# Seven whole-row taps of the last VectorE tile and three of the first TensorE conv tile, computed on ScalarE and added by accumulating transfers

## The chip, the core and the metric

The kernel runs on one core of one Trainium2 chip. A core has five engines with one instruction queue each: TensorE (PE in the profile; PEld is its weight load), VectorE (DVE), ScalarE (ACT), GpSimd (POOL) and SyncE (SP, which here only issues transfers). The engines meet through semaphores, and each queue is worked off in order: an instruction that waits holds all those behind it on its engine. Data lies in an on-chip memory of 128 partitions, matmuls write to a small accumulator memory (PSUM), and 16 DMA engines move the rest. The metric is the device time of the whole program in microseconds (us), as the median of several runs.

## What is computed

The input is x with the shape (16, 384, 32, 32): 16 images, 384 channels, 32 x 32 pixels, float32. Two residual layers follow each other; each starts with a group norm over 32 groups.

```
x = x + attention(group_norm(x))        # 8 heads of 48 channels over 1024 tokens, then a projection
w_sym = (w + rot90(w) + rot180(w) + rot270(w)) / 4
x = x + depthwise_conv_7x7(group_norm(x), w_sym, padding 3)
```

The depthwise convolution multiplies each channel with its own 7 x 7 weights, so it is a sum of 49 products, one for every shift (dy, dx) from -3 to 3, each of a shifted picture with one weight per channel. These 49 terms are called taps here. A tap with dx = 0 shifts only whole rows: it reads and writes one run of 1024, 992, 960 or 928 neighbouring values in each partition, with no gaps at row ends.

## The kernel before

**Tiles.** Channels lie on partitions, so an image is three tiles k = 0, 1, 2 of 128 channels x 1024 pixels. For every image b the attention runs on TensorE: `qk_step` (L418), `v_step` (L444), `s_step` (L469, scores, with the exponential on ScalarE at L477), `av_step` (L485) and the projection (L538, in the last image `proj_part`, L575). The result x1 (`x1s[b, k]`) is normalised into xn1 (`xn1s[b, k]`, by `conv_begin` through `Stats.apply`, L336 and L340), and the convolution adds its 49 taps onto x1, which is then stored. In the profile these names appear without digits: x is x1, xn is xn1, sum is sum2.

**Who does the convolution.** For images 0 to 13 VectorE does all 49 taps of all three tiles, one instruction per tap (`conv_tap`, L600), in turn over the active tiles so that neighbours on the queue write to different tiles. These taps fill VectorE while TensorE works on the attention of the next image. For the last two images TensorE helps with three tiles (`PE_TILES`): tile (14, 2), then (15, 2) and (15, 1). There remain (14, 0), (14, 1) and (15, 0) for VectorE; (15, 0) is called `LONE`. As taps of one tile alone would depend on each other, `tap_of_two` lets the taps of `LONE` go alternately to x1 and to a second sum `sum2`, which is started by a product at L858 and added to x1 at the end (L866). The tile is then stored by one GpSimd transfer (`conv_end`, L610).

**Convolution on TensorE.** A normalised tile is stored to DRAM (`conv_store`, L674) and loaded back in shifted copies, in two row halves h with two parts a each (`conv_load`, L681; four transfers per part, in the tail of the program two on SP and two on ScalarE's queue). `conv_on_pe` (L704) then runs, for each half, 14 taps (d0, dx), each standing for four dy: d0 = 0 holds dy = -3 to 0, d0 = 1 holds dy = 1 to 3 (and one row of zeros). Each is four matmuls of 32 output columns in the program, eight in the profile, where a float32 matmul shows as two. The pieces in which they are issued lie in `pe_conv`, filled in `x1_chains`. For (14, 2) and (15, 2) ScalarE then copies the PSUM tile (L719), an accumulating GpSimd transfer adds it to x1 (L720), and a second transfer stores x1. For (15, 1), the last one, VectorE adds the halves straight from PSUM (`conv_on_pe_half`, L727), and each half is stored by itself (L728).

**What sets the order.** The instruction order on each engine is written out by the program itself, as a planner that keeps two model clocks, `clock` for TensorE and `vclock` for VectorE. `after(wait, cost, f)` puts a piece of work into the queue `later`, due at a model time; `catch_up(to)` emits due pieces and between them as many taps as the model says fit before `to`. `applies` holds work for ScalarE, which `act_slot` emits where TensorE leaves it room. The order is fixed at build time; at run time only semaphores act. In the last image `fast_finish` (the projection's second half, the division, the statistics of x1) and `fast_end` follow; then the loop at L1253 alternates pieces of the TensorE convolution with VectorE work until nothing is left. `opool`, `npool` and `epool` are rings of 6, 6 and 8 tiles: a new tile takes the place of the oldest of its ring and waits until that is free.

Of the kernel before, what the change touches and what calls it, by code (L numbers as in the profile page):

```python
# [44 lines left out]
def kernel(  # L45
# [25 lines left out]
    nc = tc.nc  # L71

    B, C, H, W = x.shape
    N = H * W
    NK = C // P
# [3 lines left out]
    HALF = N // 2  # L79
    KS = w_conv.shape[2]  # L80
    PAD = KS // 2
# [12 lines left out]
    wsym = consts.tile([P, NK, KS, KS], F32, name="wsym")  # L94
# [15 lines left out]
    def run(general):  # L110
        tag = "g" if general else "f"
        with ExitStack() as stack:
# [23 lines left out]
            xns, x1s, qks, os_, accs, es, xn1s = {}, {}, {}, {}, {}, {}, {}  # L136
# [2 lines left out]

            PE_TILES = [(B - 2, PE_K[0])] + [(B - 1, k) for k in PE_K]  # L140
            LONE = (B - 1, 0)

            def flat(t):
                return t.rearrange("p h n -> p (h n)")
# [25 lines left out]
            late, pps = {}, {}  # L170
# [415 lines left out]
                )  # L586


            def region(*ds):
                return [(slice(max(0, -d), H - max(0, d)), slice(max(0, d), H - max(0, -d))) for d in ds]  # L590

            def conv_begin(st, b, k, engine):
                xn1s[b, k] = npool.tile([P, N], F32, tag="xn1", name=f"xn1_{b}_{k}")
                st.apply(xn1s[b, k], x1s[b, k], k, engine)

            def conv_tap(b, k, dy, dx, dst=None):
                (oy, iy), (ox, ix) = region(dy, dx)
                dst = x1s[b, k] if dst is None else dst
                acc = dst.rearrange("p (h w) -> p h w", w=W)[:, oy, ox]
                nc.vector.scalar_tensor_tensor(  # L600
                    acc,
                    xn1s[b, k].rearrange("p (h w) -> p h w", w=W)[:, iy, ix],
                    wsym[:, k, dy + PAD, dx + PAD : dx + PAD + 1],
                    acc,
                    ALU.mult,
                    ALU.add,
                )

            def conv_end(b, k):
                nc.gpsimd.dma_start(  # L610
                    out[b, k * P : (k + 1) * P].rearrange("p h w -> p (h w)"), x1s.pop((b, k))
                )
# [63 lines left out]
            def conv_load(b, k, h, a):  # L676
# [11 lines left out]
                    )  # L688
                shs[b, k, h, a] = t

            def conv_on_pe(b, k, h, first, last):
                if (b, k) not in pss:
                    pss[b, k] = psum(f"ps_conv_{b}_{k}")
                order = sorted(
                    ((d0, dx) for d0 in range(2) for dx in range(-PAD, PAD + 1)),
                    key=lambda t: t[1] != 0,
                )
                for n, (d0, dx) in enumerate(order):
                    if not first <= n < last:
                        continue  # L700
                    _, (ox, ix) = region(0, dx)
                    for i in range(SH):
                        src = shs[b, k, h, i // 2][:, i % 2, 0 : ROWS * W]
                        nc.tensor.matmul(  # L704
                            pss[b, k][CH * i : CH * (i + 1), h, :].rearrange(
                                "p (y x) -> p y x", x=W
                            )[:, :, ox],
                            lhsT=mats[k][:, i, d0 * KS + dx + PAD, :],
                            rhs=src.rearrange("p (y x) -> p y x", x=W)[
                                :, SH * d0 : SH * d0 + H // 2, ix  # L710
                            ],
                            start=(n == 0),
                            stop=(n == len(order) - 1),
                        )

            def conv_on_pe_end(b, k):
# [53 lines left out]
            if general:  # L770
                for b in range(B):
                    if b:
                        load_x(b)
                    st = Stats(f"x_{b}")
# [18 lines left out]
                    st = Stats(f"x1_{b}")  # L793
# [17 lines left out]
            clock, vclock, last_image, catching = 0.0, 0.0, 1e9, False  # L811
            later, count = [], 0
# [18 lines left out]

            def tap():

                while len(active) < NK and chains:
                    active.append([*chains.popleft(), 0])
                if not active:
                    return 0.0
                b, k, n = active[0]
                if (b, k) == LONE:
                    active.append(active.pop(0))  # L840
                    return tap_of_two(b, k, active[-1])
                took = us_tap(*TAPS[n])
                conv_tap(b, k, *TAPS[n])
                c = active.pop(0)
                c[2] += 1
                if c[2] < len(TAPS):
                    active.append(c)
                else:
                    conv_end(b, k)
                return took  # L850

            def tap_of_two(b, k, c):

                n = c[2]
                c[2] += 1
                if n == 1:
                    late["sum2"] = opool.tile([P, N], F32, tag="o", name=f"sum2_{b}_{k}")
                    nc.vector.tensor_scalar(  # L858
                        late["sum2"], xn1s[b, k], wsym[:, k, PAD, PAD : PAD + 1], None, ALU.mult
                    )  # L860
                elif n < len(TAPS):

                    tn = n if n > 1 else 1
                    conv_tap(b, k, *TAPS[tn], late["sum2"] if n % 2 else None)
                else:
                    nc.vector.tensor_tensor(x1s[b, k], x1s[b, k], late["sum2"], ALU.add)  # L866
                    active.remove(c)
                    conv_end(b, k)
                return (950 + 128) / 955

            def catch_up(to):
                nonlocal vclock, catching
# [47 lines left out]
            applies = deque()  # L920
# [142 lines left out]
            st = Stats("x_0")  # L1063
# [56 lines left out]
            def conv_piece():  # L1120
                nonlocal clock
                b, k, h, first, last = pe_conv.popleft()
                while (b, k, h, 1) not in shs and pe_loads:
                    loads(1)
                conv_on_pe(b, k, h, first, last)
                clock += 6.2 * (last - first) / KS
                if last == 2 * KS:
# [48 lines left out]
            for b, n0, size in [  # L1176
# [74 lines left out]
            vclock = clock  # L1251
# [57 lines left out]
```

## Time and profile before

| what | value |
|---|---|
| time, median of 3 runs | 2926.08 us (2924.81 to 2926.97) |
| time of the profiled execution | 2926.36 us |
| its span (first to last instruction) | 2924.6 us |
| TensorE busy | 2895.0 us, 99% |
| VectorE busy | 2580.3 us, 88% |
| ScalarE busy | 1441.0 us, 49% |
| GpSimd busy | 254.2 us, 9% |
| last matmul of the attention's projection ends | 2832.1 us |
| last matmul of the convolution ends | 2906.3 us |
| last VectorE instruction ends | 2915.0 us |

All times inside an execution are counted from the start of its span. The busy share of an engine is a mean over the whole program; the changed code runs in the last 220 us, of which the last 80 us, after the attention of image 15, matter most. So the answers of the trace for these windows say more than the totals.

### The profile page before, as it was taken

How to read it: one execution, taken by the hardware profiler on the slowest of the kernel's cores; microseconds unless marked ns; L12 is line 12 of the kernel's file. 1: busy time of each engine (PE TensorE's matmuls, PEld its weight loads, DVE VectorE, ACT ScalarE, POOL GpSimd, SP SyncE). 2: the span in 40 equal slices, each digit the busy share in tenths (PEclk: the TensorE clock that was granted, in tenths of full speed). 3: DMA queues.
4: the chain of work that ended last, by engine and by line, in shares of the span. 5: the costliest groups of instructions: out<-in, count | busy, mean ns of one | idle time of the engine just before them, and what ended most of it. 6: DMA issues, size and time to landing. Idle time of an engine off the chain costs nothing.

```text
span 2924.6 us, 30111 instructions
## 1 busy us (share of the span) xinstructions
PE 2895.0 (99%) x11442; PEld 1164.5 (40%) x11442; DVE 2580.3 (88%) x2571; ACT 1441.0 (49%) x1721; POOL 254.2 (9%) x400
## 2 busy tenths in 40 slices
PE   8999999999999999999999999999999999999997
PEld 4343343433434343343433434343343434434332
DVE  5312999989899898999989899898999989899988
ACT  2545445464454655445464454556445464554520
POOL 3111004010100101000010100101010010100000
PEclk9999999999999999999999999999999999999999
DMA  7422022120312203012220302203022220302314
GB/s 281 131 29 62 16 35 76 37 68 23 68 29 43 69 21 84 16 35 69 42 63 23 72 29 39 70 21 84 16 41 64 43 62 24 80 24 35 104 53 128
DMA packets 72059, 168.93 MB, mean 58 GB/s; under 512 B 30288, under 2 KB 32224, under 8 KB 70368
## 3 DMA queue, kind: packets, MB, share of 16 engines
q0 software_dynamic: 32688, 109.34, 14.7%
q1 hardware_dynamic: 37936, 54.94, 7.4%
q10 hardware_dynamic: 1280, 2.62, 0.3%
q8 instruction: 92, 1.51, 0.2%
q14 instruction: 63, 0.52, 0.1%
HBM read 118.61 MB, written 28.72 MB: 50 GB/s over the span
## 4 chain that ended last, share of the span: by engine, by line
PE 92%; issue 5%; DVE 2%; DMA 0%; POOL 0%; ACT 0%; POOLq 0%
PE ps_s L469 29%; PE acc L485 29%; PE ps_qk L418 17%; PE ps_v L444 9%; PE ps_proj L538 8%; DVE x L600 1%; DVE sum L600 1%; DMA x<-in_x 0%; PE warm L1060 0%; PE ps_st_x L308 0%; ACT qk L425 0%; POOL v L180 0%; POOL qk L434 0%; POOL sc_x L329 0%; POOL x L1241 0%
## 5 line engine op out<-in xcount | busy, mean ns | idle before, releaser
L600 DVE SCALAR_TENSOR_TENSOR x<-xn,wsym,x 128x899 f32<-128x899 f32 (+9 forms) x2181 | 2375.7, 1162 | 138.7 <-ACT xn L340 138.7
L477 ACT ACTIVATE e<-ps_s 128x1024 f32<-128x1024 f32 x1024 | 952.4, 1051 | 52.2 <-PE ps_s L469 49.1
L469 PE MATMUL ps_s<-qk 48*128 48x512 f32 x4096 | 914.8, 596 | 1.3 <-ACT qk L425 1.1
L485 PE MATMUL acc<-e,v 128*64 128x512 f32 x4096 | 907.2, 595 | 0.0
L469 PEld LDWEIGHTS ps_s<-qk 48*128 48x128 f32 x4096 | 375.9, 185 | 536.4 <-ACT e L477 259.6
L485 PEld LDWEIGHTS acc<-e,v 128*64 128x64 f32 x4096 | 283.0, 137 | 608.2 <-issue 600.8
L418 PE MATMUL ps_qk<-x,wqk 128*128 128x512 f32 x1152 | 508.7, 598 | 2.4 <-DVE x L336 2.4
L496 ACT COPY o<-acc 128x512 f32<-128x512 f32 x128 | 75.1, 587 | 604.7 <-PE acc L485 604.7
L418 PEld LDWEIGHTS ps_qk<-x,wqk 128*128 128x128 f32 x1152 | 217.2, 191 | 290.1 <-issue 287.6
L444 PE MATMUL ps_v<-wv,x 128*128 128x384 f32 x768 | 252.0, 488 | 0.0
L538 PE MATMUL ps_proj<-o,wp 128*128 128x512 f32 x540 | 234.2, 592 | 0.0
L425 ACT COPY qk<-ps_qk 128x1024 f32<-128x1024 f32 x96 | 96.9, 1009 | 263.6 <-PE ps_qk L418 263.6
L553 POOL DMA_DIRECT2D x<-in_x x45 | 39.4, 875 | 1803.0 <-ACT x L546 1424.3
L444 PEld LDWEIGHTS ps_v<-wv,x 128*128 128x128 f32 x768 | 144.6, 190 | 109.6 <-ACT e L477 12.1
L538 PEld LDWEIGHTS ps_proj<-o,wp 128*128 128x128 f32 x540 | 102.6, 190 | 126.0 <-issue 119.6
L453 ACT COPY v<-ps_v 128x384 f32<-128x384 f32 x128 | 55.1, 483 | 185.5 <-PE ps_v L444 185.5
L546 ACT ACTIVATE x<-ps_proj,bp 128x1024 f32<-128x1024 f32 x45 | 50.2, 1114 | 182.7 <-PE ps_proj L538 182.7
L521 DVE TENSOR_TENSOR o<-o,inv 128x1024 f32<-128x1024 f32 x63 | 76.8, 1219 | 51.0 <-DMA inv<-inv 46.5
L340 ACT ACTIVATE xn<-x,sc_x 128x1024 f32<-128x1024 f32 x46 | 53.8, 1231 | 80.3 <-DMA sc_x<-gr_x 57.0
L704 PE MATMUL ps_conv<-sh,mat 128*32 128x464 f32 (+3 forms) x672 | 69.2, 570 | 1.9 <-DVE x L727 1.9
L363 DVE BATCH_NORM_STATS2 bs_all<-xs 128x6 f32<-128x512 f32 x84 | 52.2, 683 | 18.2 <-DMA xs<-in_x 18.2
L510 DVE RECIPROCAL rec<-sums 128x16 f32<-128x16 f32 x63 | 15.3, 243 | 53.6 <-DMA sums<-sum 53.5
(123 smaller groups left out, 556.6 us busy)
## 6 DMA issues: line engine op xcount, KB each, us to landing
x<-in_x POOLq DMA_DIRECT2D x90, 512.0 KB, 5.6
inv<-inv SPq DMA_DIRECT2D x126, 256.0 KB
out<-x POOLq DMA_DIRECT2D x47, 512.0 KB, 3.8
xs<-in_x POOLq DMA_DIRECT2D x42, 512.0 KB, 6.5
qk<-qk POOLq DMA_DIRECT2D x96, 128.0 KB, 5.8
o<-o SPq DMA_DIRECT2D x90, 64.0 KB
sh<-xd SPq DMA_DIRECT2D x32, 160.0 KB
x<-in_x SPq DMA_DIRECT2D x6, 512.0 KB
```

Of the source, the lines that this page charges most:

```text
L418: nc.tensor.matmul(ps[:, h, :], lhsT=wqk[:, k, s, t, :], rhs=xns[b][:, k, h * HALF : (h + 1) * HALF], start=(k == 0), stop=(k == NK - 1),)
L425: nc.scalar.copy(halves(qks[u][:, s, :]), ps)
L444: nc.tensor.matmul(ps[:, j, 0:C], lhsT=xns[b][:, k, t * P : (t + 1) * P], rhs=wv[:, k, :], start=(k == 0), stop=(k == NK - 1),)
L453: nc.scalar.copy(dst.rearrange("p (h d) -> p h d", d=D + 1)[:, :, 0:D], ps[:, j, 0:C].rearrange("p (h d) -> p h d", d=D),)
L469: nc.tensor.matmul(ps[:, j, :], lhsT=qks[u][r, 1, i * P : (i + 1) * P], rhs=qks[u][r, 0, h * HALF : (h + 1) * HALF], start=True, stop=True,)
L477: nc.scalar.activation(es[n], ps, AF.Exp, scale=SCALE)
L485: nc.tensor.matmul(accs[u, h][64 * j : 64 * j + 64, :], lhsT=v_of(u, i, j), rhs=e[:, j, :], start=(i == 0), stop=(i == NT - 1),)
L496: nc.scalar.copy(os_[u][:, h * HALF : (h + 1) * HALF], accs.pop((u, h)))
L521: nc.vector.tensor_tensor(os_[u], os_[u], invs.pop(u), ALU.mult)
L538: nc.tensor.matmul(ps[:, h, :], lhsT=wp[:, t, o * P : (o + 1) * P], rhs=os_[NP * b + t][:, h * HALF : (h + 1) * HALF], start=(t == 0), sto ...
L600: nc.vector.scalar_tensor_tensor(acc, xn1s[b, k].rearrange("p (h w) -> p h w", w=W)[:, iy, ix], wsym[:, k, dy + PAD, dx + PAD : dx + PAD + 1],
L704: nc.tensor.matmul(pss[b, k][CH * i : CH * (i + 1), h, :].rearrange("p (y x) -> p y x", x=W)[:, :, ox], lhsT=mats[k][:, i, d0 * KS + dx + ...
```

## The change

It takes the dx = 0 taps of two tiles off the engines that did them, and it stores the last tile in another way.

- `ROWS_ONLY` names the taps: dy = 1, 2, 3 of tile (14, 2), which is TensorE's first, and all seven dy of `LONE`. `taps_of` and `pe_taps` leave them out of VectorE's and TensorE's lists; on TensorE that is the one pair (d0, dx) = (1, 0) in each of the two halves.
- `product` computes such a tap on ScalarE: one `activation` with a per-channel scale over a run of whole rows. For tile (14, 2) `rows_early` puts three products into `applies`; they write into the tiles in which xn1 of image 15 will lie later (`spare`), and GpSimd transfers with `accum_op=ALU.add` add them to x1 of (14, 2).
- For `LONE`, `lone_sums` writes the product dy = 0 into `sum2` and dy = 1 into a third sum `sum3`; `lone_rows` writes the other five into five tiles of `epool`, and `add_step` issues five accumulating transfers into `sum3`, planned 8 us apart.
- The end of `LONE` becomes: `sum2 += sum3`, then `x1 += sum2` in two halves, each stored by its own transfer, one on SP and one on ScalarE's queue, in place of one addition and one GpSimd transfer.
- In the last image xn1 of tile 0 is computed by ScalarE and no longer by GpSimd.
- `vclock -= 5.0` in `x1_chains` of image 14 lets the planner put more taps ahead of the other VectorE work that follows.

```diff
+            ROWS_ONLY = {PE_TILES[0]: (1, 2, 3), LONE: range(-PAD, PAD + 1)}
+            def taps_of(b, k):
+                return [t for t in TAPS if t[1] or t[0] not in ROWS_ONLY.get((b, k), ())]
...
+            def product(dst, b, k, dy):
+                rows, src = ((slice(i.start * W, i.stop * W)) for i in region(dy)[0])
+                nc.scalar.activation(
+                    dst[:, rows],
+                    xn1s[b, k][:, src],
+                    AF.Identity,
+                    scale=wsym[:, k, dy + PAD, PAD : PAD + 1],
+                )
+                return dst[:, rows], rows
...
             def conv_begin(st, b, k, engine):
-                xn1s[b, k] = npool.tile([P, N], F32, tag="xn1", name=f"xn1_{b}_{k}")
+                xn1s[b, k] = spare.pop((b, k), None) or new_xn1(b, k)
...
+            PE_TAPS = [(d0, dx) for d0 in range(2) for dx in range(-PAD, PAD + 1)]
+            PE_TAPS.sort(key=lambda t: t[1] != 0)
+            def pe_taps(b, k):
+                return [t for t in PE_TAPS if t != (1, 0) or (b, k) not in ROWS_ONLY]
...
             def tap_of_two(b, k, c):
                 n = c[2]
                 c[2] += 1
-                if n == 1:
-                    late["sum2"] = opool.tile([P, N], F32, tag="o", name=f"sum2_{b}_{k}")
-                    nc.vector.tensor_scalar(
-                        late["sum2"], xn1s[b, k], wsym[:, k, PAD, PAD : PAD + 1], None, ALU.mult
-                    )
-                elif n < len(TAPS):
-                    tn = n if n > 1 else 1
-                    conv_tap(b, k, *TAPS[tn], late["sum2"] if n % 2 else None)
+                taps = taps_of(b, k)
+                if n < len(taps):
+                    conv_tap(b, k, *taps[n], late["sum2"] if n % 2 else None)
+                elif n == len(taps):
+                    assert not adds
+                    dst = late["sum2"]
+                    nc.vector.tensor_tensor(dst, dst, late["sum3"], ALU.add)
                 else:
-                    nc.vector.tensor_tensor(x1s[b, k], x1s[b, k], late["sum2"], ALU.add)
+                    for h in range(2):
+                        cols = slice(h * HALF, (h + 1) * HALF)
+                        dst = x1s[b, k][:, cols]
+                        nc.vector.tensor_tensor(dst, dst, late["sum2"][:, cols], ALU.add)
+                        (nc.sync, nc.scalar)[h].dma_start(
+                            out[b, k * P : (k + 1) * P].rearrange("p h w -> p (h w)")[:, cols], dst
+                        )
                     active.remove(c)
-                    conv_end(b, k)
...
+            def add_rows(b, k, t, rows):
+                dst = late["sum3"] if (b, k) == LONE else x1s[b, k]
+                nc.gpsimd.dma_start(dst[:, rows], t, accum_op=ALU.add)
+            def rows_early(b, k, n, dy):
+                t, rows = product(spare[B - 1, n % NK], b, k, dy)
+                add_rows(b, k, t, rows)
+            def lone_sums(b, k):
+                product(late["sum2"], b, k, 0)
+                product(late["sum3"], b, k, 1)
+            def lone_rows(b, k):
+                for dy in (-1, 2, -2, 3, -3):
+                    e = epool.tile([P, 2, HALF], F32, tag="e", name=f"tap_{dy}")
+                    adds.append((b, k, *product(flat(e), b, k, dy)))
+                add_step(now())
...
             def x1_chains(b, st):
+                nonlocal vclock
                 on_pe = [t for t in PE_TILES if t[0] == b]
                 for k in range(NK - 1, -1, -1):
-                    conv_begin(st, b, k, (nc.gpsimd, None, nc.vector)[k] if b == B - 1 else None)
+                    conv_begin(st, b, k, nc.vector if (b, k) == (B - 1, NK - 1) else None)
                     if (b, k) in on_pe:
                         conv_store(b, k)
-                        cuts = (0, KS, KS + 2, KS + 4, 2 * KS) if b == B - 2 else (0, KS, 2 * KS)
+                        cuts = (0, KS, KS + 2, KS + 4) if b == B - 2 else (0, KS)
+                        cuts = (*cuts, len(pe_taps(b, k)))
                         pe_conv.extend((b, k, 0, *c) for c in zip(cuts, cuts[1:]))
-                        pe_conv.extend((b, k, 1, n, n + KS) for n in (0, KS))
+                        pe_conv.extend(((b, k, 1, 0, KS), (b, k, 1, KS, cuts[-1])))
+                if b == B - 1:
+                    lone_sums(*LONE)
+                    after(2.5, 0.0, lambda: lone_rows(*LONE))
+                if b == B - 2:
+                    vclock -= 5.0
+                    for k in range(NK):
+                        spare[B - 1, k] = new_xn1(B - 1, k)
+                    for n, dy in enumerate(ROWS_ONLY[PE_TILES[0]]):
+                        applies.append(
+                            (
+                                clock + 9.0 + 7.0 * n,
+                                1.3,
+                                lambda n=n, dy=dy: rows_early(*PE_TILES[0], n, dy),
+                            )
+                        )
...
             def fast_end(b):
+                assert not applies
+                for key in ("sum2", "sum3"):
+                    late[key] = opool.tile([P, N], F32, tag="o", name=key)
+                nc.gpsimd.memset(late["sum3"][:, N - W :], 0.0)
```

More of the change, by code (lines that the diff above doesn't have):

```diff
@@ L586, in residual, with new_xn1 @@
                 )
+            spare = {}
+            def new_xn1(b, k):
+                return npool.tile([P, N], F32, tag="xn1", name=f"xn1_{b}_{k}")
+            def product(dst, b, k, dy):
[7 more added lines that the diff above has]
+                return dst[:, rows], rows
             def region(*ds):
@@ L693, in conv_on_pe @@
                     pss[b, k] = psum(f"ps_conv_{b}_{k}")
-                order = sorted(
-                    ((d0, dx) for d0 in range(2) for dx in range(-PAD, PAD + 1)),
-                    key=lambda t: t[1] != 0,
-                )
-                for n, (d0, dx) in enumerate(order):
+                taps = pe_taps(b, k)
+                for n, (d0, dx) in enumerate(taps):
                     if not first <= n < last:
@@ L712, in conv_on_pe @@
                             start=(n == 0),
-                            stop=(n == len(order) - 1),
+                            stop=(n == len(taps) - 1),
                         )
@@ L841, in tap @@
                     return tap_of_two(b, k, active[-1])
-                took = us_tap(*TAPS[n])
-                conv_tap(b, k, *TAPS[n])
+                taps = taps_of(b, k)
+                took = us_tap(*taps[n])
+                conv_tap(b, k, *taps[n])
                 c = active.pop(0)
                 c[2] += 1
-                if c[2] < len(TAPS):
+                if c[2] < len(taps):
                     active.append(c)
@@ L855, in tap_of_two @@
                 c[2] += 1
-                if n == 1:
-                    late["sum2"] = opool.tile([P, N], F32, tag="o", name=f"sum2_{b}_{k}")
-                    nc.vector.tensor_scalar(
-                        late["sum2"], xn1s[b, k], wsym[:, k, PAD, PAD : PAD + 1], None, ALU.mult
-                    )
-                elif n < len(TAPS):
-                    tn = n if n > 1 else 1
-                    conv_tap(b, k, *TAPS[tn], late["sum2"] if n % 2 else None)
-                else:
-                    nc.vector.tensor_tensor(x1s[b, k], x1s[b, k], late["sum2"], ALU.add)
+                taps = taps_of(b, k)
@@ L867, in tap_of_two, with add_step @@
                     active.remove(c)
-                    conv_end(b, k)
                 return (950 + 128) / 955
+            adds = deque()
+            def add_step(due):
+                nonlocal count
+                add_rows(*adds.popleft())
+                if adds:
+                    due += 8.0
+                    count += 1
+                    heapq.heappush(later, (due, count, 0.0, lambda: add_step(due)))
+            def add_rows(b, k, t, rows):
+                dst = late["sum3"] if (b, k) == LONE else x1s[b, k]
+                nc.gpsimd.dma_start(dst[:, rows], t, accum_op=ALU.add)
@@ L1126, in conv_piece @@
                 clock += 6.2 * (last - first) / KS
-                if last == 2 * KS:
+                if last == len(pe_taps(b, k)):
                     loads(2)
```

## The prediction

> **What bounds the kernel now.** I read the page's chain first, then the busy time by stretches at the end, then the timeline by engine. Part 4 of the page says who sets the end over the whole program:
>
> ```profile
> PE 92%; issue 5%; DVE 2%; DMA 0%; POOL 0%; ACT 0%; POOLq 0%
> ```
>
> That is a mean. The stretches (engine columns: PE, PEld, DVE, ACT, POOL, then clock, DMA share, GB/s) show the hand-over:
>
> ```profile
> 2880.00:2900.00 20.00, 18.58 (x184) 5.79 (x176) 20.00 (x19) 1.01 (x1) 1.98 (x3) 1.00 0.58 156
> 2900.00:2925.00 25.00, 5.82 (x56) 1.70 (x56) 14.97 (x15) 0.00 (x0) 1.07 (x2) 0.72 0.12 46
> ```
>
> TensorE is full up to 2898.6 us; after that VectorE is the full one, and ScalarE is idle. Timeline of the end:
>
> ```profile
> 2832.05 5.98 PE L704 MATMUL ps_conv<-sh,mat 128*32 128x512 f32 x56
> ...
> 2900.47 5.82 PE L704 MATMUL ps_conv<-sh,mat 128*32 128x464 f32 x56 [1.89 <-DVE x L727]
> ...
> 2899.74 0.67 DVE L727 TENSOR_TENSOR x<-ps_conv,x 128x512 f32<-128x512 f32 x1
> ...
> 2912.07 0.67 DVE L727 TENSOR_TENSOR x<-ps_conv,x 128x512 f32<-128x512 f32 x1
> 2912.67 1.07 DVE L600 SCALAR_TENSOR_TENSOR x<-xn,wsym,x 128x841 f32<-128x841 f32 x1
> 2913.78 1.23 DVE L866 TENSOR_TENSOR x<-x,sum 128x1024 f32<-128x1024 f32 x1
> ...
> 2915.30 0.53 POOL L610 DMA_DIRECT2D out<-x  x1 [14.05 <-DVE x L866]
> ```
>
> VectorE ends 8.7 us after TensorE (2906.29), then 9.6 us pass to the end of the span. Note the 1.89 us: TensorE's last piece waits until VectorE has added the first half of (15, 1), though it writes the other half. The wait is for the whole PSUM tile.
>
> [...]
>
> **The changed kernel's order.** In its built instruction list the first L727 of (15, 1) now stands behind all pieces of the convolution: TensorE no longer waits for it, but it waits for the very last matmul, since the tile is waited for as a whole; the second L727 has no wait left and is VectorE's last instruction. Behind the first stand three taps, sum2 += sum3, two half additions and the second L727. So the end is TensorE's end plus this block.
>
> **Part by part.**
>
> *Early products (dy 1, 2, 3 of (14, 2)).* Slots on ScalarE, with idle time before each row:
>
> ```profile
> 2719.58 1.01 ACT L425 COPY qk<-ps_qk 128x1024 f32<-128x1024 f32 x1 [4.75 <-PE ps_qk L418]
> 2724.73 1.01 ACT L425 COPY qk<-ps_qk 128x1024 f32<-128x1024 f32 x1 [4.14 <-PE ps_qk L418]
> ...
> 2738.82 0.59 ACT L496 COPY o<-acc 128x512 f32<-128x512 f32 x1 [5.53 <-PE acc L485]
> ```
>
> One product lies between the first two copies, two before the third. [...] L340 with two pointers took 1.23. [...] so TensorE does not notice: 0. Their target tiles come free with image 13's last taps, stored from 2713.3 to 2715.3, 5 us before. Their three GpSimd transfers hold up the qk copies (2715.8) by some 7 us and the x loads (2727.0) by some 10; these are used after 2780 and at 2829.5: 0. [...]
>
> *TensorE's removed pair.* Two groups of eight matmuls; 5.98/7 = 0.854 us per group: -1.71 us. The wait for L727 goes: -1.89. TensorE's end: 2906.29 - 3.60 = 2902.7.
>
> *What may delay TensorE.* It reaches (15, 2) at 2856.75 instead of 2858.45. The first loads for it cannot start earlier (they wait for xn1's store, 2849.3) and their bytes end about here (same columns):
>
> ```profile
> 2855.00:2856.00 1.00, 1.00 (x12) 0.27 (x8) 1.00 (x2) 0.00 (x0) 0.00 (x0) 1.00 0.75 167
> 2856.00:2857.00 1.00, 1.00 (x16) 0.40 (x12) 1.00 (x2) 0.00 (x0) 0.00 (x0) 1.00 0.03 5
> ```
>
> The first accumulating transfer (product done at about 2852.5) shares the DMA engines for their last 2 us. Value taken +0.4, ends 0 and 2.0 (2.0 would be one more late load of the three groups that follow, each needed 11.6 us after its predecessor). TensorE's end: 2903.1.
>
> *VectorE's queue up to there.* Seven row taps leave: 1.16 + 1.16, 1.13 + 1.13, 1.09 + 1.09 (start to start at 992, 960, 928 values) and L858's 0.68, together 7.4. The vclock shift moves three taps of image 14 (3.1 us) in front of the divisions of the last image, where VectorE had idle time for them:
>
> ```profile
> 2803.28 3.36 DVE L566 RECIPROCAL inv<-ps_sum 128x512 f32<-128x512 f32 x1 [4.60 <-PE ps_sum L564]
> ```
>
> With 3.1 of 4.60 us filled, L566 starts no later. And LONE's first tap waits no more for GpSimd's 2.68 us xn1, now 1.25 us on ScalarE (it stood 0.8 us). So VectorE comes to the first L727 at about 2898.2, and then stands for 4.9 us. None of these 11 us counts; this gain is lost to the new wait.
>
> *The block after it.* From the rows above: pick-up 0.05, L727 0.60, taps 1.07 + 1.03 + 1.08, sum2 += sum3 1.23 (as L866), halves 0.61 + 0.61, L727 0.67: 6.95. VectorE ends at 2910.05 instead of 2915.01: -4.96.
>
> *sum3 in time?* Landings of the accumulating L720 (last number, us after issue), at 2877.0 and 2884.6:
>
> ```profile
> x<-conv POOLq DMA_DIRECT2D x1, 512.0 KB, 5.2
> x<-conv POOLq DMA_DIRECT2D x1, 512.0 KB, 8.7
> ```
>
> Five links, each waiting on GpSimd for the one before, and for (14, 2)'s L720 and store between the third and fourth: 2852.5, 2860, 2867, then L720 at about 2874, store 2881, link four 2882, link five 2889.5, landed at 2896. Needed at 2906.9: 10.9 us to spare, 0. Behind link five stand L720 and the store of (15, 2): landed at about 2902; the half of (15, 1) is hidden likewise.
>
> *The last stores.* Before, 9.6 us from L866's end to the span's end, with 512 KB through GpSimd. Now three of 256 KB, the last on SP, which starts 0.03 us after its L727 (2912.77 against 2912.74 before). Smaller, and without GpSimd's issue at the end: between 0 and -2.3 (7.3 left if SP alone sets it: 0.4 for the issue, and as SP's queue stood before, 2.8 for its branch from 2913.2, 0.5 for the waits from 2916.0, 3.6 from 2920.9 to the end). Taken -1.85.
>
> Sum: -4.96 - 1.85 = -6.8 us. The profiled execution (2926.36, span 2924.6, 1.8 around it) would become 2919.6; it lies 0.3 above the median 2926.08, so I predict 2919.3. Its own range, from TensorE's -0.4 to +1.6 and the store's -0.45 to +1.85: 2918.4 to 2922.8.
>
> **Rivals.** *The wait is only for the half's own matmuls*, and VectorE runs through: it ends at 2915.01 less 7.4 (row taps), 3.1, 0.8, plus 1.23 for the new addition, at about 2904.9; with the same stores 2914.2 us. For it: the first half's matmuls end by 2891.5. Against it: the listed wait, and the 1.89 us in the trace of before. Chance 0.07.
>
> *Loads late.* The accumulations meet each group of loads and TensorE loses more than 1 us, in several places: 2920.2 to 2924. For it: DMA share 1.0 from 2851 to 2855; against it: the later groups ended some 4 us before use. Chance 0.19.
>
> *Slower: the chain of accumulations on GpSimd.* One mechanism, place: GpSimd's queue from 2852. Links start at 2852.5; with t from one start to the next landing, link five lands at about 2854 + 5t (link four also waits for (14, 2)'s store), and VectorE's 3.1 us and a landing of 3.3 follow: 2860.5 + 5t. Before, the last store landed at 2919.5, so t = 11.8 us decides, and from there each us costs five: 2932 at 13. For it: five links in a row amid loads; against: 5.2 and 8.7 were for 512 KB, links have at most 496. Chance 0.08.
>
> The change failing to take effect (products stall ScalarE in image 15) has 0.02, near no change.
>
> **How the numbers follow.** What a measurement can tell here is 0.2%, 5.85 us: faster is below 2920.2. The forecast has 0.64; 0.07 of that ends above 2920.2. Faster: 0.57 + 0.07 = 0.64. Same: 0.07 + 0.16 of late loads + 0.02 = 0.25. Slower: 0.08 + 0.03 of very late loads = 0.11. The range 2916.5 to 2923.5 leaves out the first rival (0.07), the slower one (0.08) and 0.04 of late loads.
>
> **What would show it.** Right: L727's first addition starting right after the last matmul, with 4 to 5 us idle before it, no idle time on TensorE before its last piece, the last VectorE end 7 us after TensorE's. Wrong: idle time named "DMA sh" on TensorE; an idle L888 (sum2 += sum3) waiting for a transfer; taps between 2800 and 2844 shifting L566; GpSimd's or another's store landing last.

## The result, and the profile after

The kernel after takes 2917.31 us (median; 2915.78 to 2918.17) against 2926.07 us for the kernel before: the ratio is 0.997, with a 95% interval of 0.996 to 0.998, and 8.76 us are gone. The prediction was 2919.3 us, with a range of 2916.5 to 2923.5. The profiled execution took 2917.47 us, its span is 2915.7 us (before 2926.36 and 2924.6).

The chain of the page (part 4) is of no use in this trace: it breaks off at 2906.73 us, after eight pieces. The end is read from the stretches and the timeline instead. The stretches of the kernel after (columns: the length, then PE, PEld, DVE, ACT, POOL busy us, clock, DMA share, GB/s):

```profile
2880.00:2900.00 20.00, 20.00 (x204) 8.06 (x198) 17.95 (x17) 1.01 (x1) 3.75 (x5) 1.00 0.75 177
2900.00:2916.00 16.00, 2.90 (x30) 0.80 (x19) 6.91 (x8) 0.00 (x0) 0.56 (x1) 0.73 0.25 93
```

In the kernel before, VectorE was full in the first of these stretches and TensorE was not. Here it is the other way round: TensorE is full up to its end at 2902.90, and VectorE has 2.05 us of idle time. The timeline of the end (start us, us, engine, line, operation; in brackets the idle time ahead and who ended it) shows where it stands:

```profile
2831.96 5.90 PE L729 MATMUL ps_conv<-sh,mat 128*32 128x512 f32 x56
...
2856.68 46.22 PE L729 MATMUL ps_conv<-sh,mat 128*32 128x512 f32 x447
...
2902.93 0.69 DVE L752 TENSOR_TENSOR x<-ps_conv,x 128x512 f32<-128x512 f32 x1 [4.99 <-PE ps_conv L729]
2903.54 1.14 DVE L621 SCALAR_TENSOR_TENSOR sum<-xn,wsym,sum 128x899 f32<-128x899 f32 x1
2903.93 0.56 POOL L753 DMA_DIRECT2D out<-x  x1 [4.90 <-DVE x L752]
...
2906.82 1.23 DVE L888 TENSOR_TENSOR sum<-sum,sum 128x1024 f32<-128x1024 f32 x1
2908.08 1.29 DVE L894 TENSOR_TENSOR x<-x,sum 128x512 f32<-128x512 f32 x2
...
2909.29 0.68 DVE L752 TENSOR_TENSOR x<-ps_conv,x 128x512 f32<-128x512 f32 x1
2909.40 0.39 ACTq L895 DMA_DIRECT2D out<-x  x1
2910.00 0.36 SPq L753 DMA_DIRECT2D out<-x  x1
```

(L729 is the matmul of `conv_on_pe`, L704 before; L752 and L753 are the addition and the store of `conv_on_pe_half`, L727 and L728 before.) The long TensorE row is its last two tiles, (15, 2) and (15, 1), 224 matmuls each (one matmul is in a row of its own, not shown); they run without idle time. VectorE comes to the first addition at 2897.94, stands for 4.99 us until the last matmul, and needs 7.04 us from its start to VectorE's end at 2909.97. After that 5.7 us pass to the end of the span, where it was 9.6 before; this stretch is called the tail below.

The same point of the program lies up to 2 us earlier or later from one trace to the next (the start of TensorE's first convolution matmuls at 2830.22 to 2832.30 us), by what happens long before the change's last part. For all comparisons of steps below, times are therefore counted from the start of TensorE's first convolution matmuls, called the mark (the row "x56", the first piece of tile (14, 2); 2832.05 before, 2831.96 after):

| from there, us | TensorE ends | VectorE's stand at the first addition | VectorE ends | span ends | tail |
|---|---|---|---|---|---|
| before | 74.24 | 0 | 82.96 | 92.55 | 9.6 |
| after | 70.94 | 4.99 | 78.01 | 83.74 | 5.7 |
| difference | -3.30 | +4.99 | -4.95 | -8.81 | -3.86 |

So the gain has two parts, 4.95 us of VectorE's end and 3.86 us of the tail. The first is what was forecast (4.96). The second is twice the forecast (1.85).

### The profile page after: what moved, and what is told of

Read it like the earlier page. It is cut to its first block, busy times and chain, and to the rows that moved or that the text cites. A ratio compares the mean times of both kernels' runs of the same rounds, so it can differ in the third digit from the quotient of the medians.

```text
span 2915.7 us, 30095 instructions
## 1 busy us (share of the span) xinstructions
PE 2893.7 (99%) x11426; PEld 1168.4 (40%) x11426; DVE 2573.3 (88%) x2566; ACT 1452.0 (50%) x1732; POOL 258.2 (9%) x407
## 5 line engine op out<-in xcount | busy, mean ns | idle before, releaser
L729 PE MATMUL ps_conv<-sh,mat 128*32 128x496 f32 (+3 forms) x656 | 67.8, 569 | 0.0
L345 ACT ACTIVATE x<-x,x_sc 128x1024 f32<-128x1024 f32 x42 | 51.5, 1258 | 26.6 <-DMA x<-in_x 26.6
```

The costliest lines, as they stand in the source:

```text
L345: nc.scalar.activation(dst, src, AF.Identity, bias=self.sc[:, k, 1:2], scale=self.sc[:, k, 0:1],)
L729: nc.tensor.matmul(pss[b, k][CH * i : CH * (i + 1), h, :].rearrange("p (y x) -> p y x", x=W)[:, :, ox], lhsT=mats[k][:, i, d0 * KS + dx + ...
```

## The experiments

The theory to test: (1) in the kernel after, the end is TensorE's last matmul, then what stands behind VectorE's first addition, then a tail; (2) the tail depends on who issues the last store. Rivals: TensorE's earlier end alone is what was gained; the tail is a matter of the store's size. The kernels below were timed in three groups, each group on one chip and beside the kernel before, whose medians were 2925.54, 2925.39 and 2925.29 us; "to before" is the difference of the medians.

### What is behind VectorE's stand

In the first kernel the first half's addition is put off in the plan, behind the last tile's own taps and joins:

```
-    after(6.0, 0.7, lambda: conv_on_pe_half(b, k, h))
+    after(6.0 if h else 14.0, 0.7, lambda: conv_on_pe_half(b, k, h))
```

> The kernel after, with one change: VectorE's add of the first half of TensorE's last tile stands behind the last tile's own taps and joins instead of ahead of three taps. Theory (the end of the kernel after is VectorE's stand of 4.99 us before that add, plus all that is queued behind the add): the wait disappears, since by the time the taps and joins are done (2897.95 + 5.7 = about 2903.6) TensorE has ended (2902.90); VectorE ends at 2905.0 instead of 2909.97. But GpSimd then issues its last store, of this half, at about 2904.3, only 0.4 us later than in the kernel after (2903.93), and its drain after it ends no earlier than there (2912.6 us), so that the end is GpSimd's: 2913 to 2914, span 1.5 to 2.5 us shorter than the kernel after's 2915.7. Rival A (only VectorE's end counts, the drain of GpSimd is off the path): span 4.9 us shorter, about 2910.8. Rival B (TensorE's earlier end is what the change gained, the order of VectorE's last instructions is worth nothing): span as after, 2915.7.

Measured: 2915.5 us, span 2914.2. VectorE no longer stands, and ends at 72.93 us from the mark, 5.08 earlier than in the kernel after. But the span ends only 1.1 us earlier (1.3 us by the medians to before), less than the 1.5 to 2.5 us expected: the tail is 9.7 us. Rivals A and B are both out. The groups of the program's last line, where the engines close (queue, operation, count: ns min/median/max, first and last start us), of this kernel:

```profile
L1348 POOLq INC_SWDGE_SEM  x1: 997/997/997, 2909.0 to 2909.0; - x1
L1389 POOLq DRAIN  x3: 46/103/3335, 2910.0 to 2913.9; - x3
```

GpSimd issued its last store at 2904.22; its long drain of 3.3 us begins at 2910.0 and is over at 2913.3, and the span ends at 2914.2. SP's own waits were done by 2909.1. The second kernel moves only that store:

```
-    (nc.gpsimd, nc.sync)[h].dma_start(
+    (nc.scalar, nc.sync)[h].dma_start(
```

> As the kernel with the late add, and the store of that half is issued by ScalarE instead of GpSimd; GpSimd's last DMA is then the store of another tile at about 2898.5. Theory (wait before the add, and GpSimd's drain as the second lower end): VectorE ends at 2905.0, the tail behind it is about 5.7 as in the kernel after, span about 2910.8, so 4.9 us shorter than after and 2 to 3.4 us shorter than the same kernel with the store on GpSimd. Rival A (drain off the path): the same 2910.8, and no difference to the one with the store on GpSimd. Rival B: 2915.7.

Measured: 2911.91 us, span 2910.1, 3.6 us below the same kernel with GpSimd's store. VectorE's end is the same 72.93 from the mark; the tail is 6.5 us, where 5.7 were expected. The third kernel reaches the same end of VectorE by another way, through the dependency instead of the order:

```
-    pss[b, k] = psum(f"ps_conv_{b}_{k}")
+    if (b, k) == PE_TILES[-1]:
+        pss[b, k] = [
+            ps_o.tile([P, HALF], F32, tag="acc", name=f"ps_conv_{b}_{k}_{n}")
+            for n in range(2)
+        ]
...
-    nc.vector.tensor_tensor(dst, pss[b, k][:, h, :], dst, ALU.add)
+    nc.vector.tensor_tensor(dst, pss[b, k][h], dst, ALU.add)
```

> The kernel after, with TensorE's last tile accumulated in two PSUM tiles, one for each half, so that VectorE's first add waits only for the first half's matmuls. Theory: these end 2902.90 less about half of the 46 us of that tile, far ahead of VectorE's arrival at 2897.95, so the wait of 4.99 us becomes about 0; VectorE ends at about 2905.0, GpSimd's last store is issued at about 2899 and its drain is over by 2908, and the span is about 2910.8, 4.9 us shorter than after. Rival (the stand only moves: VectorE then waits as long for the second half, or the last store's landing and the close set the end): less than 2 us shorter.

Measured: 2912.95 us, span 2911.4. Its timeline (L760 is here the first addition):

```profile
2896.64 1.14 DVE L621 SCALAR_TENSOR_TENSOR x<-xn,wsym,x 128x899 f32<-128x899 f32 x1
2897.70 0.67 DVE L760 TENSOR_TENSOR x<-ps_conv,x 128x512 f32<-128x512 f32 x1
2898.30 1.13 DVE L621 SCALAR_TENSOR_TENSOR sum<-xn,wsym,sum 128x899 f32<-128x899 f32 x1
```

The addition starts with no idle time ahead of it, 4.88 us before TensorE ends (2902.58), so the stand in the kernel after was a wait for the second half's matmuls, which this addition does not read. VectorE ends at 72.94 from the mark. The span ends 4.1 us earlier than in the kernel after, not 4.9, since the tail is 6.7 us. (The 46 us in the expectation are the row of TensorE's last two tiles, not of one; the first half of the last tile ends a quarter of the row ahead of its end, about 11.5 us by this estimate. The argument is not touched by it.)

### What each part of the change was worth

Four kernels undo one part each; that xn1 of tile 0 went to ScalarE was not undone by itself. Without the set-back of VectorE's clock in the plan, once with the two PSUM tiles and once on the kernel after itself:

```
-    vclock -= 5.0
```

> The kernel with the two PSUM tiles, and without the line that sets VectorE's clock in the plan back by 5 us, which put three taps of other tiles' work earlier into an idle stretch. Theory: without a wait near the end, VectorE's idle time earlier counts in full: the idle time at the reciprocal was 4.60 us in the kernel before and 1.67 in the kernel after, so VectorE ends about 3.0 us later than with the line, span about 2913.8. Rival (the time is given back elsewhere, since VectorE has other waits between): 0 to 1 us later.

> The kernel after without the line that sets VectorE's clock in the plan back by 5 us. In its list six taps stand behind VectorE's add of the first half, where after has three. Theory (VectorE stands before this add until TensorE's last matmul; only what is behind it counts): it arrives at 2897 to 2898 as before and stands as long, and the block behind it is three taps of 1.03 to 1.07 us longer, so VectorE ends 3.1 us later, span about 2918.8. Rival A (the prediction's text, none of VectorE's 11 us ahead of the add counts, the shift being one of them): 0, span 2915.7. Rival B (VectorE runs through, and what counts is only the idle time that the shift fills, as in the kernel with two PSUM tiles, where it was worth 1.8 us): 1.8 us longer.

Measured: 2914.7 us with the two PSUM tiles, 1.75 more than with the line; VectorE ends 3.13 us later (76.07), as the theory says, but the tail is 1.0 us shorter, so that the time moves by less. And 2920.52 us on the kernel after: 4.87 below before where the kernel after is 8.6 to 8.8 below; VectorE ends 3.34 us later (81.35), the span 3.3 us. Rivals A and B of the second are out. The reason is in these rows of the trace without the line:

```profile
2901.89 0.69 DVE L752 TENSOR_TENSOR x<-ps_conv,x 128x512 f32<-128x512 f32 x1 [5.19 <-PE ps_conv L729]
2902.50 1.08 DVE L621 SCALAR_TENSOR_TENSOR x<-xn,wsym,x 128x841 f32<-128x841 f32 x1
```

The stand is as long as in the kernel after (5.19 against 4.99), because three taps that the plan had put ahead of it are now behind it: six taps follow instead of three.

The six row taps of the last tile go back to VectorE (ScalarE's products for them, their transfers and the join of the sums are left out):

```
-    ROWS_ONLY = {PE_TILES[0]: (1, 2, 3), LONE: range(-PAD, PAD + 1)}
+    ROWS_ONLY = {PE_TILES[0]: (1, 2, 3), LONE: (0,)}
...
```

> The kernel after with the six row taps of VectorE's last tile (dy -3 to 3 but 0) back on VectorE, without ScalarE's products for them, the five accumulating transfers and the joining of the two sums; ScalarE still starts the sum with dy 0. In its list nine taps stand behind VectorE's add of the first half, where after has three. Theory (only what is behind the stand counts): VectorE arrives at the add as in after, within 1 us, and the block behind is six taps longer (6.4 to 6.6 us) less 1.26 of the join: VectorE ends 5.2 us later, span about 2920.9. Rival A (TensorE's end sets all, VectorE's row taps were free): 0. Rival B (all of the taken work counts, [...] no stand): 6.5 to 7 us longer.

Measured, with the kernel after run beside it:

> The kernel after once more, beside the next three kernels, as their base. Ratio to before 0.997 as in the first runs, 8.5 to 9 us shorter; span about 2915.

The kernel after took 2916.66 us, ratio 0.9971 (0.996 to 0.9981); the one with the row taps 2921.68 us, 5.02 more. VectorE's end is 83.41 from the mark, against 78.28 in the kernel after of this group: 5.13 later. The row of the stand, in the kernel with the row taps:

```profile
2901.60 0.69 DVE L752 TENSOR_TENSOR x<-ps_conv,x 128x512 f32<-128x512 f32 x1 [4.93 <-PE ps_conv L729]
```

Again the stand keeps its length, and the whole difference is behind it. Rivals A and B are out. (The 6.5 to 7 us of rival B were an estimate; in the kernel before the six row taps are 1.09 to 1.16 us each from start to start, 6.8 together.) Last, TensorE's pair (1, 0) of its first tile goes back, without the three early products:

```
-    ROWS_ONLY = {PE_TILES[0]: (1, 2, 3), LONE: range(-PAD, PAD + 1)}
+    ROWS_ONLY = {LONE: range(-PAD, PAD + 1)}
...
-    for n, dy in enumerate(ROWS_ONLY[PE_TILES[0]]):
+    for n, dy in enumerate(()):
```

> The kernel after, with the three early products of TensorE's first tile and their transfers left out and that tile's pair of groups back on TensorE. In its list two taps, not three, stand behind VectorE's first add. Theory: TensorE ends 1.71 us later, at 2904.6, and the block behind is one tap of 1.05 shorter: VectorE ends 0.65 us later, span about 2916.4. Rival A (each us of TensorE counts in full): 1.7 us longer. Rival B (the early products and transfers delay TensorE by as much as they save): TensorE ends at 2902.9 still, span 1 us shorter.

Measured: 2918.03 us, 7.36 below before, so 1.3 to 1.4 above the kernel after; from the mark, TensorE ends at 73.08 (1.87 to 2.14 later than in the two traces of the kernel after), VectorE at 79.09 (0.81 to 1.08 later).

```profile
2904.16 0.69 DVE L752 TENSOR_TENSOR x<-ps_conv,x 128x512 f32<-128x512 f32 x1 [6.01 <-PE ps_conv L729]
2904.77 1.12 DVE L621 SCALAR_TENSOR_TENSOR x<-xn,wsym,x 128x870 f32<-128x870 f32 x1
2905.80 1.09 DVE L621 SCALAR_TENSOR_TENSOR sum<-xn,wsym,sum 128x841 f32<-128x841 f32 x1
```

The stand is 1.02 us longer than in the first trace of the kernel after (0.76 longer than in the second) and one tap of about 1.05 us fewer is behind it, as the theory says. The medians, 1.3 to 1.4 us apart, cannot tell 0.65 from 1.7 us. The traces can: VectorE's end moves by one tap less than TensorE's. Rival B, early products that cost as much as they save, is out.

The parts do not add up to the 4.95 us of VectorE's end: each is the worth of one part with the others in place, together 9.2 to 9.6 us, and the stand of 4.99 us takes from what they give.

Is TensorE's wait of 1.89 us in the kernel before worth anything by itself? The two PSUM tiles, put into the kernel before:

> The kernel before, with TensorE's last tile accumulated in two PSUM tiles, so that TensorE's last piece no longer waits 1.89 us for VectorE's add of the first half. Theory (VectorE sets the end in before, 8.7 us behind TensorE): TensorE ends 1.9 us earlier and the time is the same, within 0.4 us. Rival (TensorE sets the end there): 1.9 us shorter.

Measured: 2925.81 us, ratio to before 1.0001 (0.9993 to 1.001). The wait is gone, TensorE's last two tiles are one row (`2858.73 45.71 PE ...`), TensorE ends 2.10 us earlier from the mark, and VectorE ends at 82.95 as before. TensorE's earlier end was worth nothing while VectorE set the end; in the kernel after it counts, since it ends VectorE's stand.

### The tail

Two kernels, one for each side. The kernel after with its last store on GpSimd:

```
-    (nc.gpsimd, nc.sync)[h].dma_start(
+    (nc.gpsimd, nc.gpsimd)[h].dma_start(
```

> The kernel after, with one change: its last store (256 KB, the second half of TensorE's last tile) is issued by GpSimd instead of SP. Theory (the tail behind VectorE's end is set by which engine issues the last DMA: GpSimd's close takes about 9.5 us from its last issue, with a drain of 2.8 to 3.3 us in it): tail 9.3 to 9.7 us instead of 5.7, span about 2919.5, 3.6 to 4 us longer than after. Rival A (the prediction's: most of the gain at the tail is the smaller store): tail about 7.7, span 2917.7, 2 us longer. Rival B (the queue doesn't matter): 2915.7.

And the kernel before with its last store, still whole, on SP:

```
-            def conv_end(b, k):
-                nc.gpsimd.dma_start(
+            def conv_end(b, k, queue=nc.gpsimd):
+                queue.dma_start(
...
-                    conv_end(b, k)
+                    conv_end(b, k, nc.sync)
```

> The kernel before, with one change: its last store, still whole (512 KB), is issued by SP instead of GpSimd. Theory: VectorE ends at 2915.0 as in before, the tail is 5.7 to 6.7 us instead of 9.6, span 2920.7 to 2921.7, so 3 to 4 us shorter than before. Rival A (the size of the last store sets the tail): no gain, span 2924.6. Rival B (both share in it): 1 to 2 us shorter.

Measured: 2920.66 us, 4.0 above the kernel after (by their differences to before), and 2922.39 us, 3.0 below before (ratio 0.999, 0.9983 to 0.9996, so 1.2 to 5.0 us; its tail in the trace decides against the 1 to 2 us of rival B). With the kernels before and after this makes a table of four tails, VectorE's end to the span's end:

| last store | 512 KB | 256 KB |
|---|---|---|
| by GpSimd | 9.6 (before) | 9.7 |
| by SP | 6.3 | 5.7 (after) |

Who issues it is worth 3.3 to 4.0 us. The size is worth at most 0.6 us with SP (6.3 against 5.7); these lie between SP's branch and the step after it (3.6 us with 512 KB, 3.0 with 256 KB) and are within what this step varies between kernels (2.8 to 4.0). With GpSimd the two tails are equal, but this does not show that the size is worth nothing there, as the count below says. The closing rows of the kernel before, then those of the kernel after, show why the issuer counts:

```profile
L1264 POOLq COMPARE_BRANCH  x1: 61/61/61, 2915.8 to 2915.8; - x1
L1264 POOLq INC_SWDGE_SEM  x1: 856/856/856, 2920.1 to 2920.1; - x1
L1305 SPq EVENT_SEMAPHORE  x14: 17/28/28, 2920.9 to 2924.5; - x14
L1305 POOLq DRAIN  x3: 46/103/2762, 2921.0 to 2924.3; - x3
```

```profile
L1348 POOLq INC_SWDGE_SEM  x1: 997/997/997, 2908.2 to 2908.2; - x1
L1348 SPq COMPARE_BRANCH  x1: 50/50/50, 2910.4 to 2910.4; - x1
L1348 SPq EVENT_SEMAPHORE  x8: 17/17/17, 2913.4 to 2914.0; - x8
L1389 SPq EVENT_SEMAPHORE  x14: 17/28/28, 2914.0 to 2915.6; - x14
L1389 POOLq DRAIN  x3: 46/103/3335, 2909.3 to 2915.4; - x3
```

GpSimd closes in a row of steps that start only after its last issue: a branch (from there to the semaphore step 4.3 us before, 4.0 with the late addition, 3.2 in the kernel after with its last store on GpSimd), the semaphore step of 0.86 to 1.02 us, a drain of 2.8 to 3.4 us. Before, all of that stood behind VectorE's last addition. After, GpSimd's last issue is at 2903.93, its long drain is over at 2912.6, and SP's own close (2913.4 to 2915.6) is what ends last.

The length of the semaphore step and of the drain follows the number of transfers that GpSimd issues in the whole program (the sum of its issue counts in each trace):

| GpSimd's transfers | kernel | semaphore step, us | long drain, us |
|---|---|---|---|
| 380 | before, last store on SP | 0.84 | 2.68 |
| 381 | before (also with two PSUM tiles) | 0.86 | 2.76 |
| 383 | after, row taps on VectorE | 0.90 | 2.92 |
| 385 | after, pair back on TensorE | 0.93 | 3.09 |
| 387 | after, late addition, its store on ScalarE | 0.98 | 3.25 |
| 388 | after, and four of its variants | 1.00 | 3.34 |
| 389 | after, last store on GpSimd | 1.02 | 3.42 |

```profile
L1305 POOLq DRAIN  x3: 46/103/2680, 2904.6 to 2919.9; - x3
L1389 POOLq DRAIN  x3: 46/102/3417, 2914.3 to 2918.3; - x3
```

(These are the drains of the first and the last row.) Each transfer more is about 0.08 us of drain and 0.02 us of the step, whether it carries 512 KB (first two rows) or 256 KB (last two), and whether it is issued in the last 70 us (the five of the row taps) or 175 us and more ahead of the end (the three early ones). Between the two tails with GpSimd's last store there are 8 transfers, so 0.82 us of close that the kernel with 256 KB has more; without them its tail would be about 8.9 us by this estimate. So the size, or what else differs between the two kernels, may be worth some 0.7 us with GpSimd too. No run here separates it.

### A version that beats both

The kernel with the late addition and its store on ScalarE was run once more, beside the kernel after:

> The kernel with the add of the first half put behind the joins and its store on ScalarE, once more, beside the kernel after. Theory: 4.9 us shorter than the kernel after (VectorE's end 5.1 us earlier by the start of the last image's convolution, the tail 0.0 to 0.8 us longer, as in its first run). Rival (its first 2911.9 was a difference of the two calls): under 3 us shorter.

Measured: 2912.2 us, 4.46 below the kernel after of the same group and 13.1 below before (ratio 0.9956, 0.9942 to 0.9969). Its end:

```profile
2900.75 1.23 DVE L888 TENSOR_TENSOR sum<-sum,sum 128x1024 f32<-128x1024 f32 x1
2902.01 1.29 DVE L894 TENSOR_TENSOR x<-x,sum 128x512 f32<-128x512 f32 x2
2902.73 0.36 SPq L895 DMA_DIRECT2D out<-x  x1
2903.22 1.28 DVE L752 TENSOR_TENSOR x<-ps_conv,x 128x512 f32<-128x512 f32 x2
```

VectorE runs through; TensorE had ended at 2902.35, 0.87 us ahead of the first of the two additions.

## Why the prediction was right, and where it was not

*TensorE's end.* Forecast -3.2 us (the pair -1.71, the wait -1.89, late loads +0.4), measured -3.30. The pair took 1.71 us: from the mark to the long row of the last two tiles 24.72 instead of 26.43. The wait is gone. The last two tiles took 46.22 us where 45.92 were due (47.81 less 1.89), so 0.30 us more. No idle time of TensorE is listed in them, and the row is no shorter in the kernels that leave out the last tile's transfers (46.63 us) or the early ones (46.65). So no run ties these 0.30 us to late loads; the term of +0.4 is not shown.

*The new wait.* Forecast: arrival 2898.2, stand 4.9 us. Measured: 2897.94 and 4.99. The rival that the wait is only for the half's own matmuls was wrong for this kernel and became an experiment: with two PSUM tiles VectorE ends at 2904.72, and that rival had said 2904.9.

*The block behind it.* Forecast 6.95 us from TensorE's end, measured 7.07.

*"None of these 11 us counts."* This sentence of the prediction is wrong, though no number was taken from it. Of VectorE's saved time (7.4 + 3.1 + 0.8 less the join's 1.23, about 10.1 us), the stand took 4.99 back and 5.1 arrived; VectorE's end moved 4.95. The set-back of the clock alone, called worthless there, gives 3.3 us, and the row taps 5.1. Work that left VectorE's queue ahead of the addition let the plan put other taps there that would have stood behind it, so that the block behind shrank and the stand kept its length. The sum came out right because the block was counted from the new instruction order.

*Steps costed at nothing.* The early products are hidden, as the row of ScalarE's idle time before its copy shows (5.53 us before):

```profile
2720.40 1.12 ACT L602 ACTIVATE xn<-xn,wsym 128x992 f32<-128x992 f32 x1
...
2732.95 2.11 ACT L602 ACTIVATE xn<-xn,wsym 128x960 f32<-128x960 f32 x2
2738.73 0.59 ACT L501 COPY o<-acc 128x512 f32<-128x512 f32 x1 [3.67 <-PE acc L490]
```

One product takes 1.12 us for 992 values, and the next two together 2.11; ahead of the copy behind the first product 3.12 us of idle time remain (4.14 before). That they would fit was the author's estimate. Taken at the 1.23 us that L340 took for 1024 values in the kernel before, one and two products are 1.23 and 2.46 us, less than 4.14 and 5.53. On GpSimd the first of their transfers stood 6.32 us for its product, with the qk copies behind it on the queue: these are issued at 2722.38, where it was 2715.83 before (6.55 us later, forecast some 7), and the x loads at 2740.03 instead of 2726.98 (13.05 later, forecast some 10). TensorE's first convolution matmuls start at 2831.96 all the same (2832.05 before).

The chain of accumulations, the slower rival, was far from deciding (rows of the transfers: last number is us from issue to landing):

```profile
sum<-tap POOLq DMA_DIRECT2D x1, 464.0 KB, 9.1
sum<-tap_-3_13741 POOLq DMA_DIRECT2D x1, 464.0 KB, 4.3
```

The last was issued at 2891.20 and landed at 2895.5; forecast 2896, needed at 2906.8. The link of 9.1 us is the longest; by the prediction's sum 11.8 us each would have been needed to cost anything. (That sum has the last store of the kernel before land at 2919.5; its trace has 3.7 us from the issue at 2915.30, so 2919.0, and 11.7 us.)

*The tail, the term that was mis-sized.* Forecast -1.85 us with a bound of -2.3, measured -3.86. The mechanism named in passing ("without GpSimd's issue at the end") was right, the size was not, and the bound was too narrow. It came from SP's queue as it stood before: 0.4 + 2.8 + 0.5 + 3.6 = 7.3 us. The last term is the failing one: the 3.6 us from 2920.9 to the end were taken as SP's own, but in them SP stood for GpSimd's drain (2921.0 to 2923.8). Where no drain is late, these rows of SP take 1.7 us (2914.0 to 2915.7 after, 2918.5 to 2920.2 in the kernel before with its last store on SP), and the tail is 0.4 + 3.0 + 0.6 + 1.7 = 5.7. The prediction took the rows of SP alone; the row of GpSimd's drain stands beside them in the same view of the kernel before, at the same time, and would have shown it.

*The sum.* -4.96 - 1.85 = -6.8 forecast; -4.95 - 3.86 = -8.8 measured. The measured 2917.31 us lies below the 2918.4 to 2922.8 that the forecast's own terms allowed, and inside the stated range of 2916.5 to 2923.5 only because that one reaches lower; for the tail, this is luck and not a forecast.

What stays open: the tail was 6.5 to 6.7 us, not 5.7, in three traces without a late GpSimd store (two of the kernel with the store on ScalarE, one of that with two PSUM tiles). There 3.9 to 4.0 us, and not 3.0, pass from SP's branch to the step after it (from ScalarE's 3.7 to 4.0). No run tells why.

## What to carry to other kernels

Where an engine stands for another near the end of a program, cost the instructions queued behind the stand, and ask what a planner moves across it: work taken from anywhere ahead can come back as work pulled forward from behind. A dependency on a whole PSUM tile can be the stand itself; two tiles, or the same addition some instructions later, removed VectorE's 5 us here, of which 3.8 to 4.9 reached the time where no late store by GpSimd took their place. Look at which engine closes last: a last store by GpSimd cost 3.3 to 4.0 us more than one by SP, at both sizes tried. Where GpSimd closes last, each of its transfers also counts there, with 0.10 us in these kernels.

## What the runs showed of the hardware that was not expected

GpSimd's closing steps grow by 0.10 us for each transfer that it issued earlier, and not with the bytes: 3.52 us for 380 transfers, 4.43 for 389. Only counts between these were run, so nothing is shown for programs with few transfers or many.

The early accumulating transfers and the set-back of the plan's clock together slowed a small chain elsewhere. SP's issue of the store of a reciprocal and of the load back, before and then after:

```profile
2722.92 0.34 SPq L512 DMA_DIRECT2D inv<-rec  x1
2724.35 1.13 SPq L515 DMA_DIRECT2D inv<-inv  x2
```

```profile
2725.66 0.34 SPq L517 DMA_DIRECT2D inv<-rec  x1
2730.50 1.13 SPq L520 DMA_DIRECT2D inv<-inv  x2
```

From the one to the other 4.84 us pass instead of 1.43. With the early products and their transfers left out it is 1.41; without the set-back of the clock, but with the transfers, it is 1.43. So it took both: counted from the mark, the store is issued 2.8 us later than before, 2.9 with the transfers left out, and not later without the set-back. How the two together hold up the load back is not shown. VectorE's use of it at 2735.04 has no idle time ahead of it in this trace, and 0.29 us in the second trace of the kernel after, so it cost next to nothing. But the load back is issued some 6 us later than before; the prediction had not named this chain among those that the three transfers pass.
